# Four gate banks with a transpose each, and input products once per 16 steps, in a recurrent step of an LSTM-and-experts kernel

## The chip, the cores and the metric

One core of a Trainium2 chip runs the program. The metric is the device time of one execution in microseconds. Five engines work side by side, each in the order of its own instruction stream: TensorE (PE in the profile; its weight loads are listed as PEld), VectorE (DVE), ScalarE (ACT), GpSimd (POOL) and SyncE (SP, which here only starts DMAs). They wait for each other through semaphores. Matmul results land in PSUM, which has eight banks per partition; everything else lies in SBUF.

## The reference

The input `x` has shape (2, 1024, 256). An LSTM runs over its 1024 steps for both sequences, and a layer of experts runs on the result. Both add to `x`. All numbers are float32.

```python
xW = jnp.einsum('ntd,dk->tnk', x, Wx) + b              # gates in the order i, f, o, g
def step(carry, xw_t):
    prev_h, prev_c = carry
    a = xw_t + prev_h @ Wh                             # (2, 256) @ (256, 1024)
    i, f = sigmoid(a[:, :H]), sigmoid(a[:, H:2*H])
    o, g = sigmoid(a[:, 2*H:3*H]), tanh(a[:, 3*H:])
    next_c = f * prev_c + i * g
    next_h = o * tanh(next_c)
    return (next_h, next_c), next_h
x = x + hs                                             # h0 = cond_1024, c0 = 0
# then, on every token: two shared experts (SiLU gated, 512 wide) and eight routed
# experts (GELU, 256 wide), of which a router takes the best two
x = x + experts(x)
```

Each of the 1024 steps needs the `h` of the step before, so the steps can't overlap. The experts of a token need only that token's `h`.

## The kernel before

**The step.** The 256 hidden units are two halves, `m` = 0 and 1, of 128 units. A step is written out in the loop `for t in range(T)` (line 728). TensorE multiplies `h` by `Wh` in 32 products (line 747): for each of the 8 entries of `BLOCKS` (line 69) four products, one for each 32-row strip `q`. An entry is `(k, m, pair)`: which half of the old `h` is multiplied, which half of the units is made, and which two of the four gates. Every product is float32 and leaves two weight loads and two matmuls in the trace (32 columns of weights, 64 columns of moving data), so a step has 64 of each. The products of the half `m` accumulate into one PSUM bank `ps[m]`, 128x64.

**The window.** `h_window` hands TensorE 32 columns of which 2 are the two sequences' `h` and the others are zero, at a place that moves with the step. So one bank collects the rows of several steps, and products of other steps add zeros to them. In the kernel before, 16 of the 32 rows belong to one pair of gates and 16 to the other (`PAIR`), which gives 8 steps (`TH`) before a fresh bank is needed. `gates_ps` has two buffers for each half, so the next 8 steps' bank can be prepared.

**Input products.** `x @ Wx + b` is computed ahead for blocks of 128 steps into `inputs`. `inject` (line 654) adds it into a gate bank by a product with the identity: eight products for 8 steps, spread over the steps, into the next bank (`nxt`).

**After the products.** VectorE transposes each half's bank in 32x32 blocks within the same bank (`transpose`, line 787), which puts units on partitions. ScalarE then makes three gates with one sigmoid (line 790) and `g` with a tanh (line 791). VectorE computes `f*c` (line 794), copies `g` to a scratch tile `seen` so that the scan itself need wait for one semaphore only (line 798), and forms `c` with a scan (line 799). ScalarE makes `tanh(c)` (line 807), VectorE makes `h` (line 810). VectorE's order in a step is: both transposes; then `forget`, `seen`, scan of half 0; the same of half 1; then the two `h`.

**Fill.** The experts' work and the input products are queued in `Fill` as small units. `run_pe` gives TensorE some of them after the 32 products of a step, at most `ROOM` = 4 in cost (a 128x256 product with 256 tokens costs 2). `GROUPS` says how many steps' tokens go through the experts together, `PACES` over how many steps that work is spread. ScalarE's and VectorE's parts of it run at the end of a step within budgets (line 824: 1.0, line 835: 0.6). When no unit is left, a product `busy` of 128x256 on the identity may be issued; whether it is, is decided at the first step of each 8 (`spare`, line 760) and holds for the 8.

**Instruction counting.** `fill.issued` counts TensorE's instructions (4 per product, plus the extra wait instructions that `WAITS` lists by step). `inject` is moved and split so that a multiple of `FETCH` = 256 doesn't fall just at a step's start. The profile lists these fetches as a DMA queue of its own, `q8 instruction`.

**The end.** The last 32 steps' experts can only run when the loop is over (`last_shared_down`, `last_routed_down`, `last_add`, from line 502).

Of the kernel before, what the change touches and what calls it, by code (L numbers as in the profile page):

```python
# [16 lines left out]
P = 128  # L17
# [6 lines left out]
PAIR = ROWS // 2  # L24
TH = PAIR // N
TB = 2 * TH
# [9 lines left out]
GROUPS = [128] * 3 + [32] + [128] * 4 + [64, LAST]  # L36

PACES = [128] * 7 + [56, 31, 0]
# [9 lines left out]

FETCH = 256
EARLY = 16  # L50
WAITS = (
    1, 8, 16, 24, 32, 40, 48, 56, 64, 72, 80, 88, 96, 104, 112, 120, 128, 136, 144, 149,
    152, 157, 160, 160, 165, 168, 176, 181, 184, 189, 192, 197, 200, 208, 216, 224, 232,
    240, 248, 256, 264, 272, 280, 288, 296, 304, 312, 320, 328, 336, 344, 352, 360, 368,
    376, 384, 392, 400, 408, 416, 419, 421, 423, 424, 428, 430, 432, 435, 437, 439, 440,
    440, 447, 448, 456, 464, 472, 480, 488, 496, 504, 512, 520, 528, 529, 536, 544, 552,
    560, 568, 576, 584, 592, 600, 608, 616, 624, 632, 640, 648, 656, 664, 672, 680, 688,
    688, 696, 704, 712, 720, 728, 736, 744, 752, 760, 768, 776, 784, 792, 800, 808, 816,
    824, 832, 840, 848, 856, 864, 872, 880, 888, 896, 904, 912, 920, 928, 930, 933, 935,
    936, 940, 942, 944, 947, 949, 951, 952, 956, 958, 960, 963, 965, 968, 976, 984, 992,  # L60
    999, 1000, 1004, 1006, 1008, 1011, 1013,
# [6 lines left out]

BLOCKS = [
    (0, 0, 0), (0, 0, 1), (0, 1, 0), (1, 0, 0), (1, 0, 1), (0, 1, 1), (1, 1, 0), (1, 1, 1)  # L70
# [3 lines left out]
class Fill:  # L74
# [36 lines left out]
    def run(self, queue, budget):  # L111
        while queue and queue[0][0] <= self.step and queue[0][1] <= budget:
            _, cost, fn = queue.popleft()
            budget -= cost
            fn()

# [18 lines left out]
def lstm_moe_kernel(  # L135
# [106 lines left out]
    gates_ps = ctx.enter_context(tc.tile_pool(name="gates_ps", bufs=2, space=PSUM))  # L242
# [22 lines left out]
    behind = deque([(gates_ps, "ps0"), (fill_ps, "ps_f"), (gates_ps, "ps1")])  # L265
# [20 lines left out]
    def experts(t0, S):  # L286
# [215 lines left out]
        def last_shared_down(c):  # L502
            if c < 0:
                st["down"] = bank()
                x_kqj = st["down"][:W, 0, :].rearrange("p (q k j) -> p k q j", q=Q, k=K)
                for k in range(K):
                    product(
                        x_kqj[:, k], mov[k], ident_s,
                        start=(k == 0), stop=False, skip_group_check=True,
                    )  # L510
                return
            ps, n = st["down"], NS * HS // P
            for g in range(2):
                product(
                    ps[g * W : (g + 1) * W, 0, :], st["h_s"][:, c + g, :W], w2_sb[:, c + g, :],
                    start=(c + g == 1), stop=(c + 2 == n), skip_group_check=True,
                )
            if c + 2 == n:
                fill.to_dve(0.45, lambda: begin_sum(0, ps), lag=0)
# [12 lines left out]
        def last_add(e2, ps):  # L532
            acc = st["acc", 0]
            nc.vector.scalar_tensor_tensor(  # L534
                acc, ps[:, 0, :], st["gates"][:, e2 : e2 + 1], acc, ALU.mult, ALU.add
            )
            fill.let_go()
            if e2 == E // 2 - 1:
                both = bank()[:W, 0, :]
                product(both, fold, acc, start=True, stop=True)  # L540
                total = work.tile([P, D], F32, name="y")[:W]
                nc.scalar.activation(total, both, AF.Copy)  # L542
                nc.sync.dma_start(out=out_tn[t0 : t0 + S], in_=total)
# [40 lines left out]

# [11 lines left out]
    def h_window(t, k, pair):  # L596
        at = EDGE + t % TB * ROWS - N * (t % TH) - pair * PAIR
        return hs[t // TB % 2][:, k, at : at + ROWS]

# [7 lines left out]
    def pairs(blk):  # L607
        flat = blocks[blk].rearrange("p (h c) w -> p h (c w)", c=2)
        return flat.rearrange("p h (g c r) -> p h g c r", c=2, r=PAIR)

    def keep_inputs(blk, tile_, w0, w1, ps):
        h, c = divmod(tile_, 2)
        nc.scalar.activation(  # L613
            pairs(blk)[:, h, w0 // PAIR : w1 // PAIR, c, :],
            ps[:, : w1 - w0].rearrange("p (g r) -> p g r", r=PAIR),
            AF.Identity, bias=b_sb[:, tile_ : tile_ + 1],
        )
        made.update((blk, tile_, w) for w in range(w0, w1, PAIR))

# [34 lines left out]
    def inject(banks, grp, i, pieces=1):  # L654
        m, q = divmod(i, Q)
        blk, g = divmod(grp, XB // TH)
        assert all((blk, 4 * m + 2 * (q // 2) + c, g * PAIR) in made for c in range(2))
        for piece in range(pieces):
            w0, w1 = 64 * piece // pieces, 64 * (piece + 1) // pieces
            product(  # L660
                banks[m][0][q * ROWS : (q + 1) * ROWS, w0:w1],
                pairs(blk)[:, 2 * m + q // 2, g].rearrange("p c r -> p (c r)"),
                ident[:, q % 2 * 64 + w0 : q % 2 * 64 + w1],
                start=(piece == 0), stop=False, skip_group_check=True,
            )

    def gates_tile(m):

        a = gates_ps.tile([P, 4, P], F32, name=f"ps{m}")
        return a[:, 0, :64], a[:, 1, :64], a[:, 2:]  # L670
# [10 lines left out]

    ends, e0 = {}, 0
# [28 lines left out]
    nxt = [gates_tile(m) for m in range(K)]  # L711
    busy = nxt[0][2]
# [12 lines left out]
    for i in range(K * Q):  # L725
        inject(nxt, 0, i)
    due = 12
    for t in range(T):
        fill.step = t
        grp, u = divmod(t, TB)  # L730
        if t % TH == 0:
            cur, nxt = nxt, [gates_tile(m) for m in range(K)]
            ps, turned, busy = [a[0] for a in cur], [a[1] for a in cur], nxt[0][2]
            spare = False
# [10 lines left out]

        for k, m, pair in BLOCKS:
            for q in range(Q):
                w0 = q * D + m * P + pair * 64
                product(
                    ps[m][q * ROWS : (q + 1) * ROWS],  # L750
                    h_window(t, k, pair),
                    wh_sb[:, k, w0 : w0 + 64],
                    start=False,
                    stop=(t % TH == TH - 1 and k == K - 1 and pair == 1),
                    skip_group_check=True,
                )
        left = max(1, due - t)
        done = fill.run_pe(-(-len(fill.pe) // left), ROOM)
        if t % TH == 0:
            spare = not done  # L760
        if spare and not done:
            product(
                busy, ident, ident.unsqueeze(1).to_broadcast([P, 2, P]),
                start=(t % TH == 0), stop=False, skip_group_check=True,
            )

        if t // TH + 1 < T // TH:
            put = put if t % TH else 0
            fill.issued += WAITS.count(t)

            left = K * Q - put
            count = next(
                (n for n in range(max(0, t % TH + 1 - put), left + 1)
                 if -(fill.issued + 4 * n) % FETCH > EARLY), left)
            first = -(fill.issued + 4 * count) % FETCH
            for i in range(count):
                more = i == count - 1 and first <= EARLY
                inject(nxt, t // TH + 1, put, 2 + first // 4 if more else 1)
                put += 1

        rows = slice(N * (t % TH), N * (t % TH + 1))
        gates = [turned[m].rearrange("p (a r) -> p a r", r=PAIR)[:, :, rows] for m in range(K)]
        c_new = [cells[m][:, t % 2] for m in range(K)]
        seen = [stepp.tile([P, N], F32, name=f"seen{m}") for m in range(K)]

        def transpose(m):
            nc.vector.transpose(turned[m], ps[m])  # L787

        def squash(m):
            nc.scalar.activation(sgm[:, u, m, :, :, 1], gates[m][:, 0:3], AF.Sigmoid)  # L790
            nc.scalar.activation(gf[:, u, m, :, 0], gates[m][:, 3], AF.Tanh)  # L791
# [4 lines left out]
        def cell(m):  # L796

            nc.vector.tensor_copy(seen[m], gf[:, u, m, :, 0])  # L798
# [13 lines left out]
        for fn in (transpose, squash):  # L812
            for m in range(K):
                fn(m)
        for m in range(K):
            forget(m)
            cell(m)
            squash_cell(m)
        for m in range(K):
            output(m)  # L820
        if u == TB // 2 and t + TB < T:
            nxt_results = results()
        else:
            fill.run(fill.act, 1.0)
# [9 lines left out]
        if u < TB - 1:  # L834
            fill.run_dve(0.6)
            continue
# [91 lines left out]
```

## Time and profile before

| | us |
|---|---|
| median of 3 runs (2252.95 to 2262.92) | 2254.86 |
| the profiled execution, its own time | 2256.97 |
| span of its instructions, first to last | 2254.8 |
| TensorE busy, matmuls / weight loads | 2033.5 / 1484.8 |
| VectorE busy | 1571.3 |
| ScalarE busy | 909.5 |
| first transpose starts at | 10.16 |
| last `h` ends at | 2234.03 |

The mean granted TensorE clock is 0.996 of full speed. A matmul's duration in the trace includes the way through the array: the 64 matmuls of a step take 0.22 us each by their rows and yet are done in about 1.1 us together. "Busy 90%" of TensorE therefore says little about how much more it could take. What counts in this kernel is the length of one step, since 1023 of them follow each other between the first transpose and the last.

### The profile page before, as it was taken

The numbers are of one execution on the slowest core, as the hardware profiler recorded it, in microseconds if no ns is written. First come the engines' busy times: TensorE is split into PE (matmuls) and PEld (weight loads), VectorE is DVE, ScalarE is ACT, GpSimd is POOL, SyncE is SP. The second block draws the span as 40 slices with busy tenths as digits, with TensorE's granted clock in tenths as the row PEclk, the third lists the DMA queues.
The fourth block names the chain that finished last, engine by engine and source line by source line (L and its number), as shares of the span: only waits on it lengthen the run. The fifth ranks groups of instructions, "written<-read, shape, count | busy, mean of one in ns | idle before, by whom it ended". The sixth has DMA issues, their size and how long they took to land.

```text
span 2254.8 us, 159246 instructions
## 1 busy us (share of the span) xinstructions
PE 2033.5 (90%) x70612; PEld 1484.8 (66%) x70612; DVE 1571.3 (70%) x11041; ACT 909.5 (40%) x6487; POOL 2.7 (0%) x9
## 2 busy tenths in 40 slices
PE   8988899888989889998798899988898988989998
PEld 6666666666666666777666666666666666667787
DVE  5666667776777667777667767676676776667776
ACT  3334344433444334443344443444434344334443
POOL 0000000000000000000000000000000000000000
PEclk9999999999999999999999999999999999999999
DMA  2111100000000000000000000000000000000000
GB/s 65 35 35 35 35 28 5 5 5 7 7 5 5 5 7 7 5 7 7 5 6 5 5 5 7 7 4 5 5 7 7 4 5 5 7 7 5 5 9 7
DMA packets 15330, 23.84 MB, mean 11 GB/s; under 512 B 2864, under 2 KB 14128, under 8 KB 14640
## 3 DMA queue, kind: packets, MB, share of 16 engines
q1 hardware_dynamic: 14352, 12.62, 1.9%
q8 instruction: 552, 9.04, 1.7%
q14 instruction: 138, 1.13, 0.2%
q10 hardware_dynamic: 288, 1.05, 0.1%
HBM read 11.56 MB, written 2.10 MB: 6 GB/s over the span
## 4 chain that ended last, share of the span: by engine, by line
PE 61%; DVE 36%; issue 3%; DMA 0%; SPq 0%; ACT 0%
PE ps L255 53%; DVE ps L787 10%; DVE c L799 10%; PE ps_f L255 8%; DVE results L794 7%; DVE seen L798 6%; DVE h L810 3%; DMA wh_sb<-in_wh_dram 0%; SPq L165 0%; DVE acc L534 0%; SPq L173 0%; SPq L171 0%; SPq L170 0%; DVE acc L492 0%; ACT y L542 0%
## 5 line engine op out<-in xcount | busy, mean ns | idle before, releaser
L255 PE MATMUL ps<-wh_sb,h 128*32 128x64 f32 x65536 | 1143.8, 221 | 214.3 <-DVE h L810 210.5
L255 PEld LDWEIGHTS ps<-wh_sb,h 128*32 128x32 f32 x65536 | 975.1, 110 | 393.1 <-DVE h L810 386.8
L787 DVE STREAM_TRANSPOSE ps<-ps 128x64 f32<-128x64 f32 x2048 | 543.4, 265 | 498.5 <-PE ps L255 426.0
L790 ACT ACTIVATE results<-ps 128x6 f32<-128x6 f32 x2048 | 361.3, 176 | 1103.8 <-DVE ps L787 1009.4
L810 DVE TENSOR_TENSOR h<-results,c 128x2 f32<-128x2 f32 x2048 | 314.2, 153 | 168.4 <-ACT c L807 168.2
L807 ACT ACTIVATE c<-c 128x2 f32<-128x2 f32 x2048 | 321.5, 157 | 217.5 <-DVE c L799 181.7
L799 DVE TENSOR_TENSOR_SCAN c<-results 128x4 f32<-128x4 f32 x2048 | 358.2, 175 | 0.0
L791 ACT ACTIVATE results<-ps 128x2 f32<-128x2 f32 x2048 | 342.4, 167 | 0.0
L798 DVE COPY seen<-results 128x2 f32<-128x2 f32 x2048 | 332.8, 162 | 0.0
L794 DVE TENSOR_TENSOR results<-results,c 128x2 f32<-128x2 f32 x2048 | 319.3, 156 | 0.0
L255 PEld LDWEIGHTS ps<-ident,inputs 128*32 128x32 f32 x2090 | 124.0, 108 | 265.7 <-issue 228.4
L255 PE MATMUL ps<-ident,inputs 128*32 128x64 f32 (+2 forms) x2090 | 263.9, 230 | 0.3
L255 PE MATMUL ps_f<-x2T,w_sb 128*128 128x256 f32 (+3 forms) x640 | 173.4, 379 | 0.0
L255 PE MATMUL ps_f<-x2T,r_sb 128*128 128x256 f32 (+3 forms) x640 | 173.2, 378 | 0.0
L255 PE MATMUL ps_f<-r_sb,h_r 128*128 128x256 f32 (+1 forms) x520 | 165.9, 419 | 0.9 <-DVE acc L492 0.9
L255 PEld LDWEIGHTS ps_f<-x2T,r_sb 128*128 128x128 f32 (+1 forms) x640 | 88.5, 184 | 22.8
L255 PEld LDWEIGHTS ps_f<-x2T,w_sb 128*128 128x128 f32 (+1 forms) x640 | 86.7, 184 | 21.8 <-issue 0.2
L255 PEld LDWEIGHTS ps_f<-r_sb,h_r 128*128 128x128 f32 (+1 forms) x520 | 80.0, 184 | 23.3 <-DVE acc L492 1.3
L255 PE MATMUL ps_f<-xT_sb,wx_sb 128*128 128x256 f32 (+2 forms) x384 | 84.5, 346 | 0.3 <-ACT inputs L613 0.3
L255 PE MATMUL ps<-ident 128*128 128x256 f32 x232 | 82.8, 443 | 1.4 <-POOL ident masks.py:199 1.4
L255 PE MATMUL ps_f<-w_sb,h_s 128*128 128x256 f32 (+1 forms) x256 | 82.6, 419 | 0.0
L492 DVE SCALAR_TENSOR_TENSOR acc<-ps_f,gate,acc 128x256 f32<-128x256 f32 (+1 forms) x128 | 61.1, 478 | 1.2 <-PE ps_f L255 1.0
(87 smaller groups left out, 475.1 us busy)
## 6 DMA issues: line engine op xcount, KB each, us to landing
r_sb<-in_r_w1T_dram SPq DMA_DIRECT2D x16, 128.0 KB, 2.5
r_sb<-in_r_w2T_dram SPq DMA_DIRECT2D x16, 128.0 KB, 2.1
out_dram<-acc SPq DMA_DIRECT2D x15, 128.0 KB, 2.1
xT_sb<-in_xT_dram SPq DMA_DIRECT2D x14, 128.0 KB, 2.5
wx_sb<-in_wx_dram ACTq DMA_DIRECT2D x2, 512.0 KB, 4.3
wh_sb<-in_wh_dram SPq DMA_DIRECT2D x2, 512.0 KB, 6.2
w_sb<-in_s_w1T_dram SPq DMA_DIRECT2D x8, 128.0 KB, 2.2
w_sb<-in_s_w3T_dram SPq DMA_DIRECT2D x8, 128.0 KB, 2.2
```

The lines of the kernel that those rows point to most:

```text
L255: nc.tensor.matmul(*operands, **how)
L492: nc.vector.scalar_tensor_tensor(acc, ps, st["gate"][:, i, e : e + 1], acc, ALU.mult, ALU.add)
L787: nc.vector.transpose(turned[m], ps[m])
L790: nc.scalar.activation(sgm[:, u, m, :, :, 1], gates[m][:, 0:3], AF.Sigmoid)
L791: nc.scalar.activation(gf[:, u, m, :, 0], gates[m][:, 3], AF.Tanh)
L794: nc.vector.tensor_mul(gf[:, u, m, :, 1], sgm[:, u, m, 2, :, 1], c_prev[m][:, :, 1])
L798: nc.vector.tensor_copy(seen[m], gf[:, u, m, :, 0])
L799: nc.vector.tensor_tensor_scan(c_new[m].rearrange("p n z -> p (n z)"), sgm[:, u, m, 0].rearrange("p n z -> p (n z)"), gf[:, u, m].rearrang ...
L807: nc.scalar.activation(cells[m][:, 2, :, 0], c_new[m][:, :, 1], AF.Tanh)
L810: nc.vector.tensor_mul(h_cols(t + 1)[:, m], sgm[:, u, m, 1, :, 1], cells[m][:, 2, :, 0])
```

## The change

- **Four banks.** Each half has two gate banks, one for `f` and `g` (pair 0) and one for `i` and `o` (pair 1); `gates_ps` has one buffer of each. The host puts the gates in the order f, g, i, o (`early`).
- **No pairs in the rows.** All 32 rows of a bank belong to steps, so a bank serves 16 steps (`TB`). `TH`, `PAIR` and the buffer pairs `cur`/`nxt` are gone.
- **Order of the products.** `BLOCKS` now finishes the banks in the order (0, f g), (0, i o), (1, f g), (1, i o): after 3, 4, 6 and 8 of its entries. Old half 1 of `h` is needed from the third entry on (the fourth before).
- **Four transposes per step** instead of two, and VectorE's order becomes: transpose (0, f g), (0, i o), (1, f g), `forget(0)`, transpose (1, i o), scan of half 0, `forget(1)`, scan of half 1, the two `h`. The copies to `seen` are gone. In the built program each scan has a separate wait instruction ahead of it on VectorE, for its own engine's `forget`, while the scan itself waits for ScalarE's `i, o`.
- **ScalarE** has three activations per half instead of two: sigmoid of `f`, tanh of `g`, sigmoid of `i, o`.
- **Input products at once.** At the end of each 16th step all 16 `inject` products for the next 16 steps are issued, after at most half the usual fill.
- **Fill.** `busy` is issued in every step without fill. `ready_pe` counts what `run_pe` will issue. Groups and paces near the end, and the budgets of ScalarE and VectorE fill (0.9, 0.5), are changed.
- **Instruction counting.** `WAITS` lists about one extra wait per step, and after the fill small 32x32 products on the identity are added as padding (1436 in the built program) so that, one step ahead of the burst of input products, the next multiple of 256 is 72 to 140 instructions away.
- **The end.** The last expert sum is made, folded, copied and stored in two column halves; the residual of the last group is added by two products that lie on different rows.

The long `WAITS` table and blank lines are left out of the diff.

```diff
-TB = 2 * TH
+TB = ROWS // N
-GROUPS = [128] * 3 + [32] + [128] * 4 + [64, LAST]
-PACES = [128] * 7 + [56, 31, 0]
+GROUPS = [128] * 3 + [32] + [128] * 3 + [64] * 3 + [LAST]
+PACES = [128] * 6 + [60, 60, 48, 27, 0]
-EARLY = 16
+EARLY = 12
+STEP = 137
+FROM, UPTO = 72, 140
 BLOCKS = [
-    (0, 0, 0), (0, 0, 1), (0, 1, 0), (1, 0, 0), (1, 0, 1), (0, 1, 1), (1, 1, 0), (1, 1, 1)
+    (0, 0, 0), (0, 0, 1), (1, 0, 0), (1, 0, 1), (1, 1, 0), (0, 1, 0), (0, 1, 1), (1, 1, 1)
 ]
...
+    def ready_pe(self, count, room):
+        done, banks = 0, self.banks
+        for opens, cost, _ in self.pe:
+            if done == count or opens > banks or cost > room:
+                break
+            banks -= opens
+            room -= cost
+            done += 1
+        return done
...
-    gates_ps = ctx.enter_context(tc.tile_pool(name="gates_ps", bufs=2, space=PSUM))
+    gates_ps = ctx.enter_context(tc.tile_pool(name="gates_ps", bufs=1, space=PSUM))
...
-    def h_window(t, k, pair):
-        at = EDGE + t % TB * ROWS - N * (t % TH) - pair * PAIR
+    def h_window(t, k):
+        at = EDGE + t % TB * ROWS - N * (t % TB)
         return hs[t // TB % 2][:, k, at : at + ROWS]
...
-    def inject(banks, grp, i, pieces=1):
...
+    def inject(grp, m, pair):
+        blk, g = divmod(grp, XB // TB)
+        w = slice(g * ROWS, (g + 1) * ROWS)
+        for q in range(Q):
+            tile_ = 4 * m + 2 * (q // 2) + pair
             product(
+                ps[m][pair][q * ROWS : (q + 1) * ROWS], blocks[blk][:, tile_, w],
+                ident[:, q % 2 * 64 : q % 2 * 64 + 64],
+                start=True, stop=False, skip_group_check=True,
             )
...
+    banks = [
+        [gates_ps.tile([P, 4, P], F32, name=f"ps{m}{pair}") for pair in range(2)] for m in range(K)
+    ]
+    ps, turned = [[[a[:, j, :64] for a in b] for b in banks] for j in range(2)]
+    busy = banks[0][0][:, 2:]
...
         for k, m, pair in BLOCKS:
             for q in range(Q):
                 w0 = q * D + m * P + pair * 64
                 product(
+                    ps[m][pair][q * ROWS : (q + 1) * ROWS], h_window(t, k), wh_sb[:, k, w0 : w0 + 64],
+                    start=False, stop=(u == TB - 1 and (m, pair) in seen), skip_group_check=True,
                 )
...
-        for fn in (transpose, squash):
-            for m in range(K):
-                fn(m)
-        for m in range(K):
-            forget(m)
-            cell(m)
-            squash_cell(m)
+        transpose(0, 0)
+        squash(0)
+        transpose(0, 1)
+        squash_late(0)
+        transpose(1, 0)
+        squash(1)
+        forget(0)
+        transpose(1, 1)
+        squash_late(1)
+        cell(0)
+        squash_cell(0)
+        forget(1)
+        cell(1)
+        squash_cell(1)
         for m in range(K):
             output(m)
+        left = max(1, due - t)
+        count = -(-len(fill.pe) // left)
+        feeds = u == TB - 1 and t < T - 1
+        room = ROOM // 2 if feeds else ROOM
+        done = fill.ready_pe(count, room)
+        fill.run_pe(count, room)
+        if not done:
+            product(
+                busy, ident, ident.unsqueeze(1).to_broadcast(busy.shape),
+                start=False, stop=False, skip_group_check=True,
+            )
+        fill.issued += WAITS.count(t)
+        if feeds:
+            for m, pair in PAIRS:
+                inject((t + 1) // TB, m, pair)
+        to_go = (TB - 2 - u) % TB
+        then = -(fill.issued + to_go * STEP) % FETCH
+        short = -(-max(0, then - UPTO if then > UPTO else then + FETCH - UPTO if then < FROM else 0) // 4)
+        pads = -(-short // (to_go + 1)) if t < T - TB else 0
+        while pads or not EARLY < -fill.issued % FETCH < FETCH - 2:
+            product(
+                busy[:ROWS, 0, :ROWS], ident[:, :ROWS], ident[:, :ROWS],
+                start=False, stop=False, skip_group_check=True,
+            )
+            pads = max(0, pads - 1)
```

## The prediction

> **What bounds the kernel now.** I read first the list of costliest groups (which engine carries the step), then the chain of waits, then one undisturbed step in order of time, and last the steps that are longer than it. The chain's first line says that neither DMA nor ScalarE's or SyncE's own work fills it; it alternates between TensorE and VectorE:
>
> ```profile
> PE 61%; DVE 36%; issue 3%; DMA 0%; SPq 0%; ACT 0%
> ```
>
> One step, start and duration in us:
>
> ```profile
> 601.66 0.15 DVE L810 TENSOR_TENSOR h<-results,c 128x2 f32<-128x2 f32 x1
> ...
> 601.86 0.94 PEld L255 LDWEIGHTS ps<-wh_sb,h 128*32 128x32 f32 x64 [0.82 <-DVE h L810]
> ...
> 601.97 0.16 DVE L810 TENSOR_TENSOR h<-results,c 128x2 f32<-128x2 f32 x1 [0.16 <-ACT c L807]
> ...
> 602.69 0.60 DVE L787 STREAM_TRANSPOSE ps<-ps 128x64 f32<-128x64 f32 x2 [0.42 <-PE ps L255]
> ...
> 602.99 0.18 ACT L790 ACTIVATE results<-ps 128x6 f32<-128x6 f32 x1 [1.05 <-DVE ps L787]
> 603.07 0.17 ACT L791 ACTIVATE results<-ps 128x2 f32<-128x2 f32 x1
> 603.20 0.16 DVE L794 TENSOR_TENSOR results<-results,c 128x2 f32<-128x2 f32 x1
> 603.27 0.16 DVE L798 COPY seen<-results 128x2 f32<-128x2 f32 x1
> ...
> 603.39 0.17 DVE L799 TENSOR_TENSOR_SCAN c<-results 128x4 f32<-128x4 f32 x1
> ...
> 603.60 0.16 ACT L807 ACTIVATE c<-c 128x2 f32<-128x2 f32 x1
> ...
> 603.73 0.17 DVE L799 TENSOR_TENSOR_SCAN c<-results 128x4 f32<-128x4 f32 x1
> 603.81 0.15 DVE L810 TENSOR_TENSOR h<-results,c 128x2 f32<-128x2 f32 x1
> ```
>
> From `h` to `h` it is 2.15 us (2.153 by the exact starts of most steps). TensorE starts 0.05 after `h` of half 0, the first transpose 0.83 later, and `h` 1.12 after that. The first transpose is at 10.165, the last pair at 2232.44: 1023 steps of 2.172 on average, so 19.7 us in all lie above 2.153. Three views show where:
>
> ```profile
> 40.80:51.00 10.20, 8.07 (x230) 6.55 (x222) 4.78 (x37) 2.61 (x20) 0.00 (x0) 0.53 0.11 30
> ```
>
> This stage ran at about half the granted clock (0.53, third number from the end). Its steps 13 to 17 took 3.3 us more than five of 2.153; two like it (at 1471 and 1751) took 1.1 each: **5.5 us**.
>
> ```profile
> 1773.61 0.27 DVE L787 STREAM_TRANSPOSE ps<-ps 128x64 f32<-128x64 f32 x1 [0.17 <-PE ps L255]
> ...
> 1774.15 0.14 PEld L255 LDWEIGHTS ps<-wh_sb,h 128*32 128x32 f32 x3 [0.45 <-issue]
> ...
> 1774.49 0.27 DVE L787 STREAM_TRANSPOSE ps<-ps 128x64 f32<-128x64 f32 x1 [0.62 <-PE ps L255]
> 1774.66 0.14 DVE L794 TENSOR_TENSOR results<-results,c 128x2 f32<-128x2 f32 x1
> ```
>
> Here TensorE waited for nothing that the profile names, in the middle of the step's products. Counting TensorE's instructions, 30 such gaps (0.10 to 0.56 us) lie exactly where a new block of 256 begins, together **8.3 us**: instruction fetch. The same rows give the spacing of a transpose: the next VectorE instruction starts 0.17 after it, though it lasts 0.27.
>
> **The new step, in ns from its first transpose.** Hops read from the starts of a clean step: VectorE end to ScalarE start 33, ScalarE to VectorE 35, `h` to TensorE 52. VectorE starts its next ready instruction 84 to 92 before the end of the last: 72 after a TENSOR_TENSOR, 82 after a scan, 174 after a transpose. A scan waiting for its own engine starts 36 after that end; with a separate wait instruction ahead it is 37 + 66 = 103 (in the row of three L492 sums at 2234.14 the second starts 0.10 after the first one's end, the third 0.04 after the second's; the built program has that wait ahead of the second).
>
> TensorE: step 0 shows a restart in the middle:
>
> ```profile
> 9.66 0.60 PEld L255 LDWEIGHTS ps<-wh_sb,h 128*32 128x32 f32 x40 [0.57 <-DMA wh_sb<-in_wh_dram]
> ...
> 10.16 0.60 DVE L787 STREAM_TRANSPOSE ps<-ps 128x64 f32<-128x64 f32 x2 [2.68 <-PE ps L255]
> ```
>
> 0.500 from load to transpose with 16 loads between; the second transpose 0.334 later for 24 more, 13.9 each. The new step restarts at its 17th load, when `h` of half 1 arrives. Bank (0, f g) is complete 8 loads later: first transpose at 500 - 112 = 388 after the restart, the other banks 112, 335 and 558 after it.
>
> - Transposes: 0; 174; 348 (its bank at 335); then `forget(0)` at 522 (its sigmoid: 298, 465, +35 = 500); transpose (1, i o) at 594 (its bank at 558).
> - Scan 0: `forget(0)` ends 678, +103 = 780. `forget(1)` 862, ends 1018. Scan 1: 1018 + 103 = 1121 (its sigmoid of `i, o`: 594 + 265 + 33 = 892, ends 1064, +35 = 1099: waits 22 less).
> - `tanh` of half 1: 1121 + 174 + 33 = 1328; `h` 1519, ends 1675; TensorE restarts 1727; next first transpose **2115**.
> - `h` of half 0 stands behind scan 1: 1203, ends 1355, TensorE 1407. Its 16 loads take 195, so TensorE then stands 125 waiting for half 1. That is its cover.
>
> So removing two copies and adding two transposes costs VectorE time, and the gain is that half 0's gates no longer wait for 40 loads: 2115 against 2153, **1023 x -38 = -38.9 us**. Each ns of transpose spacing moves the step by 3 (both `forget`s and scan 1 stand behind three of them); at 187 the gain is gone.
>
> A rule stands against this row. The Trainium skill, "VectorE: DVE Perf Modes", section "The DRAIN you can't avoid", says that the next VectorE operation doesn't start until the pipe is empty. By it a transpose would hold the next for its 265, the walk would give 2467 a step and the sum some 2578 us. The row at 1774.66 has 174, and the row decides.
>
> **What else changes.**
>
> - *Clock.* In the built program before, 19 steps have neither fill nor `busy`; 12 to 15, 671 and 799 just ahead of the slow clock are among them. Afterwards there are none: **-5.5** (0 if it drops anyway).
> - *Fetch.* Before, 72 blocks begin among `h` products less than 4.0 us after the one before (by the order of the instructions, at 2.153 a step) and lose 0.107 each; 403 come later and lose 0.0016. The new program has 129 of the first kind, counted in the same way at 2.115. 62 of them follow the burst of input products, two steps on at load 27, and come some 0.5 us closer than before; I take 0.2 for these (between 0.107 and 0.6), 0.107 for 67: 19.6, less 8.3 = **+11**. Ends: 0 and 129 x 0.5 - 8 = +57.
> - *Full steps.* With two 256-wide products of fill TensorE's own time rules:
>
> ```profile
> 1001.05 0.97 PEld L255 LDWEIGHTS ps<-wh_sb,h 128*32 128x32 f32 x64
> ...
> 1002.11 0.73 PEld L255 LDWEIGHTS ps_f<-w_sb,h_s 128*128 128x128 f32 x4
> ...
> 1003.17 0.14 PEld L255 LDWEIGHTS ps<-ident,inputs 128*32 128x32 f32 x2 [0.33 <-ACT c L807]
> ```
>
>   1.06 + 1.06 = 2.12, and 0.04 for small products behind it, as here until 1003.21. 174 new steps are so full, 122 with padding: 122 x 0.045 + 52 x 0.005 = **+5.7** (0 to +14, if padding costs 0.1). Before, this was covered by 2.153.
> - *Burst.* 1.06, one fill product 0.63, 32 loads 0.45, 0.02 for padding: 2.16 in 63 steps: **+2.8** (0 to +8). The last four wait for the sigmoid of bank (1, i o), which ends before their turn.
> - *VectorE fill* had 0.72 from `h` to the transpose and has 0.60; the longest takes 0.48 - 0.08 = 0.40 after 0.07: hidden. *ScalarE* has one activation more per half, inside its waits: hidden.
> - *End.* Three L492 sums and 8 weight loads of the group before follow the last `h`, and the last group's first product comes at 2236.60. With the new pace that group's products are issued by step 1019: **-2** (0 to -3). The split at the end is inside this.
>
> Sum against the profiled execution: 2256.97 - 38.9 - 5.5 + 11.3 + 5.7 + 2.8 - 2 = 2229.4; the median of the runs lies 2.1 lower: **2227**.
>
> **Rivals.**
>
> 1. *The separate waits don't bind* (the sigmoid of half 1 does, at 1099): 22 less a step, 2205. For it: only 22 ns apart. Against: the wait sits in the same stream as its `forget`. 0.12.
> 2. *Instruction fetch becomes the bound of the burst.* The burst puts some 200 instructions into one step, so the next block is wanted earlier; before, the largest gap was 0.56. At 0.56 in all 129 places: 72 - 8 = +64 in place of 11, 2280. It turns slower from 0.36 each (47 us, which is 39 more than before). For it: it is the only stall that grows with a shorter step. Against: 39 of the 72 short intervals before show none. 0.14.
> 3. *A transpose doesn't let a transpose start early.* Only TENSOR_TENSOR behind a transpose is shown. At 200 ns: 26 x 3 = 78 more a step than forecast, 2307; from 187 the step is no shorter than before. 0.06.
> 4. *TensorE rules most steps, not 174*, by tile changes between fill, padding and products: the step stays near 2.15, about 2250. Single-fill steps need 1.06 + 0.63 + 0.04, so 0.4 is spare. 0.08.
>
> The forecast itself has 0.60, with 2208 to 2245. A measurement here tells from about 0.5% (11 us). Faster: 0.58 of the forecast, 0.12 of rival 1 and little else, 0.71; slower: rival 3, half of rival 2, some of 4: 0.17; same 0.12. The range takes rival 1 with less fetch at the low end and half of rival 2 at the high end: 2196 to 2264.
>
> **What would show it.** Right: clean steps of 2.10 to 2.13; VectorE's first two transposes 0.17 apart; scan 1 0.10 after `forget(1)` ends; a pause of 0.1 before the 17th load; no stage at half clock. Wrong: transposes 0.2 or more apart, or gaps at "issue" of 0.3 and more in the step after next behind each burst.

## The result: 1.1% slower, by instruction fetch

| | before | after |
|---|---|---|
| median of 4 runs, us | 2255.32 (2252.95 to 2262.92) | 2279.56 (2276.78 to 2290.74) |
| ratio to before (95% interval) | | 1.0111 (1.0070 to 1.0152) |
| profiled span, us | 2254.8 | 2278.1 |
| first transpose, us | 10.165 | 9.893 |
| step, most steps, us | 2.153 | 2.095 |
| step, mean of 1023, us | 2.172 | 2.191 |
| from the end of the last `h` to the end, us | 20.8 | 24.8 |

The forecast was 2227, in a range of 2196 to 2264. The two rows on the step hold the story: a step that nothing disturbs became 0.058 us shorter, more than forecast, and the mean step still became 0.019 longer. All the times in this section and below that are finer than a row shows are taken from the starts of the instructions in the trace.

The undisturbed step first. Timeline of the kernel after, start and duration in us:

```profile
603.14 0.15 DVE L851 TENSOR_TENSOR h<-results,c 128x2 f32<-128x2 f32 x1
...
603.34 1.04 PEld L324 LDWEIGHTS ps<-wh_sb,h 128*32 128x32 f32 x64
...
604.05 0.60 DVE L827 STREAM_TRANSPOSE ps<-ps 128x64 f32<-128x64 f32 x3 [0.35 <-PE ps L324]
...
604.56 0.15 DVE L837 TENSOR_TENSOR results<-results,c 128x2 f32<-128x2 f32 x1
604.63 0.26 DVE L827 STREAM_TRANSPOSE ps<-ps 128x64 f32<-128x64 f32 x1
...
604.81 0.17 DVE L840 TENSOR_TENSOR_SCAN c<-results 128x4 f32<-128x4 f32 x1
604.89 0.15 DVE L837 TENSOR_TENSOR results<-results,c 128x2 f32<-128x2 f32 x1
...
605.15 0.17 DVE L840 TENSOR_TENSOR_SCAN c<-results 128x4 f32<-128x4 f32 x1
605.23 0.15 DVE L851 TENSOR_TENSOR h<-results,c 128x2 f32<-128x2 f32 x1
```

From `h` to `h` 2.09. The 64 weight loads last 1.04 where the row of before had 0.94: the pause before the 17th load is in it. Three transposes take 0.60 together, so they overlap as the walk had it; the scan of half 1 stands 0.26 behind the start of its `forget`.

Now what ate it. The list of groups of weight loads, first the kernel before, then the kernel after (count | busy us, mean ns | idle time ahead of them and what ended it):

```profile
L255 PEld LDWEIGHTS ps<-wh_sb,h 128*32 128x32 f32 x65536 | 975.1, 110 | 393.1 <-DVE h L810 386.8 <-issue 4.3 <-DMA wh_sb<-in_wh_dram 0.6
```

```profile
L324 PEld LDWEIGHTS ps<-wh_sb,h 128*32 128x32 f32 x65536 | 1017.8, 109 | 250.3 <-DVE h L851 110.6 <-issue 57.6 <-DMA wh_sb<-in_wh_dram 0.6
```

"issue" is time in which TensorE waited for nothing that the profile names: 4.3 us before, 57.6 after. Counted by TensorE's instructions as in the prediction, 114 gaps over 0.095 us lie inside the `h` products at the place where a block of 256 begins, together 68.0 us; before there were 30 with 8.3. They are not spread evenly. With u the step's place in its 16 (the burst of input products ends u = 15), the mean step is 2.828 at u = 1 and 2.327 at u = 6; no other is above 2.22. The two make (0.733 + 0.232) x 64 = 62 us. One step u = 1, kernel after:

```profile
1345.13 0.57 PEld L324 LDWEIGHTS ps<-wh_sb,h 128*32 128x32 f32 x27 [0.22 <-DVE h L851]
...
1345.84 0.27 DVE L827 STREAM_TRANSPOSE ps<-ps 128x64 f32<-128x64 f32 x1
...
1346.50 0.59 PEld L324 LDWEIGHTS ps<-wh_sb,h 128*32 128x32 f32 x37 [0.80 <-issue]
...
1346.86 0.49 DVE L827 STREAM_TRANSPOSE ps<-ps 128x64 f32<-128x64 f32 x2 [0.75 <-PE ps L324]
```

27 loads, then nothing for 0.80, then the other 37. `h` has long been there; the second transpose waits for TensorE, and the step lasts 3.00. This is the gap of "0.3 and more in the step after next behind each burst" that the prediction named as what would prove it wrong.

The end of the kernel, after:

```profile
2253.10 0.16 DVE L851 TENSOR_TENSOR h<-results,c 128x2 f32<-128x2 f32 x1 [0.17 <-ACT c L848]
2253.57 2.04 DVE L564 SCALAR_TENSOR_TENSOR acc<-ps_f,gate,acc 128x256 f32<-128x256 f32 x4
...
2254.63 5.41 PE L324 MATMUL ps_f<-r_sb,h_r 128*128 128x256 f32 x16 [1.74 <-DVE acc L564]
...
2259.96 0.41 PE L324 MATMUL ps<-wr_sb,x2T 128*64 128x8 f32 x8
```

16 of these instructions of the group before the last are still to come after the last `h` (before: 8, in 1.99 us), they wait for a bank that four sums hold, and they run in a stage of lower clock (0.68 as the mean of 2254.6 to 2260). The last group's first product starts 6.7 us after the end of `h`, against 2.6.

### The profile page after: what moved, and what is told of

It reads as the page before. It is cut to its first block, busy times and chain, and to the rows that moved or that the text cites. A ratio compares the mean times of both kernels' runs of the same rounds, so it can differ in the third digit from the quotient of the medians.

```text
span 2278.1 us, 170316 instructions
## 1 busy us (share of the span) xinstructions
PE 2157.1 (95%) x73638; PEld 1603.6 (70%) x73638; DVE 1620.3 (71%) x11067; ACT 1085.2 (48%) x8537; POOL 2.7 (0%) x9
## 4 chain that ended last, share of the span: by engine, by line
PE 72%; DVE 20%; issue 6%; ACT 2%; DVEq 0%; DMA 0%; SPq 0%; ACTq 0%
PE ps L324 53%; PE ps_f L324 19%; DVE ps L827 11%; DVE c L840 5%; DVE results L837 2%; DVE h L851 1%; ACT results L830 1%; ACT results L831 0%; DVEq L840 0%; ACT results L834 0%; DMA wh_sb<-in_wh_dram 0%; ACT c L848 0%; DVE acc L564 0%; SPq L234 0%; ACT er L512 0%
## 5 line engine op out<-in xcount | busy, mean ns | idle before, releaser
L324 PE MATMUL ps<-wh_sb,h 128*32 128x64 f32 x65536 | 1241.1, 222 | 99.0 <-issue 40.9
L324 PEld LDWEIGHTS ps<-wh_sb,h 128*32 128x32 f32 x65536 | 1017.8, 109 | 250.3 <-DVE h L851 110.6
L827 DVE STREAM_TRANSPOSE ps<-ps 128x64 f32<-128x64 f32 x4096 | 864.7, 254 | 354.2 <-PE ps L324 314.7
L830 ACT ACTIVATE results<-ps 128x2 f32<-128x2 f32 x2048 | 352.5, 172 | 909.9 <-DVE ps L827 878.0
L324 PEld LDWEIGHTS ps<-ident 128*32 128x32 f32 (+1 forms) x3170 | 208.3, 117 | 300.3 <-ACT results L834 157.6
L834 ACT ACTIVATE results<-ps 128x4 f32<-128x4 f32 x2048 | 357.0, 174 | 56.7 <-DVE ps L827 38.0
L324 PE MATMUL ps<-ident 128*32 128x32 f32 (+1 forms) x3170 | 359.9, 224 | 13.6 <-POOL ident masks.py:199 1.4
L831 ACT ACTIVATE results<-ps 128x2 f32<-128x2 f32 x2048 | 342.3, 167 | 0.0
L837 DVE TENSOR_TENSOR results<-results,c 128x2 f32<-128x2 f32 x2048 | 308.3, 151 | 1.7 <-ACT c L848 1.7
L324 PEld LDWEIGHTS ps_f<-x2T,w_sb 128*128 128x128 f32 (+1 forms) x704 | 93.8, 184 | 22.7 <-PE ps L324 0.9
L518 DVE SCALAR_TENSOR_TENSOR h_r<-er,ps_f 128x256 f32<-128x256 f32 x126 | 52.3, 415 | 0.6 <-ACT er L512 0.6
```

Of the source, the lines that this page charges most:

```text
L324: nc.tensor.matmul(*operands, **how)
L518: nc.vector.scalar_tensor_tensor(st["h_r"][:, c + i : c + j, :W], er[:, i:j], 1.0, ps[:, i:j], ALU.add, ALU.mult)
L827: nc.vector.transpose(turned[m][pair], ps[m][pair])
L830: nc.scalar.activation(sgm[:, u, m, 2, :, 1], gates[m][0][:, 0], AF.Sigmoid)
L831: nc.scalar.activation(gf[:, u, m, :, 0], gates[m][0][:, 1], AF.Tanh)
L834: nc.scalar.activation(sgm[:, u, m, :2, :, 1], gates[m][1], AF.Sigmoid)
```

## The experiments

Two theories stood against each other: that blocks of instructions arrive too late for TensorE (fetch), or that the burst itself (16 products, the restart of four banks) makes what follows late. The runs below were on two other chips, on each of which the kernel before took 2250, not 2255; so they are compared by their ratio to it. The kernel after was not run there; by its ratio it would be 1.0111 x 2250 = 2275, with an interval of 9 us each way.

**e1: the same work, blocks begin elsewhere**

```diff
-FROM, UPTO = 72, 140
+FROM, UPTO = 72, 80
```

> The window for the start of a block in the burst step is narrowed from 72-140 to 72-80 instructions: the same work, 64 padding products more, and the blocks of 256 start some 60 instructions earlier. Fetch theory: the 0.73 us by which the step two on from the burst (u = 1) is longer than 2.095 vanishes there, and comes back in the step right behind the burst (u = 0), where a block then starts at load 60, by the starts of the instructions 2.5 us after the one before instead of 3.1: 1.0 to 1.2 us a burst; u = 11 takes over the 0.23 of u = 6, at 0.5. In all 33 to 50 us more than 2279.6: 2312 to 2330. Rival (the burst itself, its products or its restart of the four banks, makes what follows late): u = 1 stays 0.7 too long and the time stays at 2275 to 2285.

Measured: 2275.17 us, ratio 1.0116 (1.0099 to 1.0133). The stall moved to the steps that fetch names: u = 1 fell from 2.828 to 2.111, u = 6 from 2.327 to 2.116, u = 0 rose from 2.203 to 2.960 and u = 11 from 2.123 to 2.230. The step behind the burst, timeline of e1:

```profile
1339.30 0.95 PEld L324 LDWEIGHTS ps<-wh_sb,h 128*32 128x32 f32 x61
...
1340.92 0.14 PEld L324 LDWEIGHTS ps<-wh_sb,h 128*32 128x32 f32 x3 [0.67 <-issue]
...
1341.26 0.27 DVE L827 STREAM_TRANSPOSE ps<-ps 128x64 f32<-128x64 f32 x1 [0.66 <-PE ps L324]
```

Now 61 loads run, and the last 3 wait 0.67. The burst is the same as before, so it is not the burst that stops TensorE in the step after next. The size was missed: a sum of 33 to 50 us more was expected, and there is none (within those 9 us). In e1 the block ahead of the stall begins among `h` products, not in the burst; its transfer of instructions then starts 0.92 us after that and has landed at 1.99 (medians of 64), while behind a start in the burst it was 1.18 and 2.37 (63). So the stall from the shorter interval (2.56 instead of 2.97, medians of all stalled places) is 0.87 instead of 0.73, not 1.0 to 1.2. In both places TensorE goes on some 1.4 us after the landing. Why a transfer starts later behind the burst stays open.

**e2: no padding for the place of the blocks**

```diff
-        pads = -(-short // (to_go + 1)) if t < T - TB else 0
+        pads = 0
```

> No padding products to bring the blocks into step with the burst (1290 of 1436 are gone; the rule on the last 12 instructions of a step stays), so that blocks start at every place of the step in turn. Fetch theory: half of the bursts have a stall in the step behind them and half in the one after, the 0.23 at u = 6 goes, and 23 blocks fewer are fetched: 15 to 30 us less than 2279.6, 2250 to 2265. Rival (the burst itself): u = 1 stays at 2.8 us in nearly all groups, the padding was 1290 x 0.02 hidden under VectorE, 2275 to 2282.

Measured: 2229.97 us, ratio 0.9913 (0.9898 to 0.9927): 45 us less than the kernel after by the ratios, more than expected. The stalls at block starts fell by 46, so the 1290 padding products themselves cost nothing that shows. u = 0 takes 2.313 and u = 1 2.278, so the stall is shared between the two, and u = 6 is down to 2.108. The padding, which was to bring the blocks into step with the burst, put the stall into nearly every group (62 of 64) at the same bad place.

**e3: no fill in the burst step**

```diff
-        room = ROOM // 2 if feeds else ROOM
+        room = 0 if feeds else ROOM
...
-        if not done:
+        if not done and not feeds:
```

> The burst step issues no fill product and no busy product; they go to the next steps. Fetch theory: the block that starts in the burst starts 0.3 us earlier (the burst then waits for the gates' activations, not for fill), so the stall two steps on shrinks by about that: 0.3 x 62 = 19 us at most, with the 0.08 of u = 15 another 4 us; 2258 to 2275. Rival (the burst itself): only the 0.08 of u = 15 goes, 2275, and u = 1 stays at 2.83.

Measured: 2254.14 us, ratio 1.0018 (1.0009 to 1.0027). u = 1 goes from 2.828 to 2.645 (12 us in 64 groups), u = 15 from 2.217 to 2.109 (7 us); the rest, 5 us by the two traces, are small parts of other steps. The block in the burst begins earlier, and the stall two steps on is shorter by 0.18, not by the full 0.3.

**e4: padding by a list**

```diff
-        to_go = (TB - 2 - u) % TB
...
-        while pads or not EARLY < -fill.issued % FETCH < FETCH - 2:
+        for _ in range(PADS.count(t)):
             product(
                 busy[:ROWS, 0, :ROWS], ident[:, :ROWS], ident[:, :ROWS],
```

The list `PADS` stands in place of the rule and of the `WAITS` table; a step has 0 to 8 padding products by it.

> The rule for padding is replaced by a list, 534 products instead of 1436, set so that a block starts as seldom as possible among the step's h products less than 3.6 us after the one before (92 such places, 36 of them under 3.2, against 117 and 88). Nothing else differs. Fetch theory: 28 to 40 us less than 2279.6: 2240 to 2252, a little faster than the kernel before (2255), with the clean step still 2.095. Rival (the burst itself): 2275 to 2282.

Measured: 2220.09 us, ratio 0.9870 (0.9855 to 0.9885): 1.3% faster than the kernel before, and 20 us below the range expected (15, when the range is moved to a chip where the kernel before takes 2250). Its clean step is 2.100 in half of the steps and 2.096 in a quarter. The groups of weight loads, e1 to e4 in order:

```profile
L324 PEld LDWEIGHTS ps<-wh_sb,h 128*32 128x32 f32 x65536 | 1016.6, 109 | 239.3 <-DVE h L851 83.5 <-issue 54.1 <-DMA wh_sb<-in_wh_dram 0.2
```

```profile
L324 PEld LDWEIGHTS ps<-wh_sb,h 128*32 128x32 f32 x65536 | 1008.8, 110 | 585.9 <-DVE h L851 520.2 <-issue 19.5 <-ACT results L834 0.8
```

```profile
L324 PEld LDWEIGHTS ps<-wh_sb,h 128*32 128x32 f32 x65536 | 1017.3, 109 | 227.0 <-DVE h L851 101.9 <-issue 36.4 <-ACT results L831 1.1
```

```profile
L285 PEld LDWEIGHTS ps<-wh_sb,h 128*32 128x32 f32 x65536 | 1005.8, 110 | 532.0 <-DVE h L812 483.8 <-issue 3.8 <-DMA wh_sb<-in_wh_dram 0.9
```

The "issue" term runs 57.6, 54.1, 19.5, 36.4, 3.8 from the kernel after to e4, and the ratios 1.0111, 1.0116, 0.9913, 1.0018, 0.9870 follow it: from after to e4 it falls by 54 us, and 0.0241 x 2250 is 54 too; from after to e3 by 21, and 0.0093 x 2250 is 21. Less close are e2 (38 for 45 us) and e1 (3.5 for none). Counted one by one, as the 68.0 was, the stalls at block starts sum to 68.0, 62.1, 22.1, 47.1 and 5.0 us. The same step as shown above, 609, in e4:

```profile
1309.02 1.04 PEld L285 LDWEIGHTS ps<-wh_sb,h 128*32 128x32 f32 x64 [0.67 <-DVE h L812]
...
1309.73 0.60 DVE L788 STREAM_TRANSPOSE ps<-ps 128x64 f32<-128x64 f32 x3
```

All 64 loads in one row, at 1.04. The five profiles (after, e1 to e4) together give the stall as a function of the time between the starts of two blocks. Counted are blocks that begin among `h` products behind the 17th load; the interval is taken without the stall itself, and the stall is what the gap has over the usual 0.014 between two loads:

| interval, us | under 2.6 | 2.6-2.9 | 2.9-3.2 | 3.2-3.5 | 3.5-3.8 | 3.8-4.1 | over 4.1 |
|---|---|---|---|---|---|---|---|
| blocks | 56 | 35 | 304 | 79 | 73 | 845 | 465 |
| mean stall, us | 0.84 | 0.66 | 0.35 | 0.27 | 0.05 | 0.013 | 0.005 |

The interval alone doesn't decide. Each start of a block is followed by one transfer in the queue of instructions (579 and 579 in the kernel after), and when that transfer lands says more. All blocks among `h` products in all ten profiles, by the time from this landing to the moment at which the next block is wanted:

| landing to wanted, us | under 0.6 | 0.6-0.8 | 0.8-1.0 | 1.0-1.2 | 1.2-1.4 | 1.4-1.6 | over 1.6 |
|---|---|---|---|---|---|---|---|
| blocks | 96 | 71 | 100 | 148 | 256 | 420 | 3675 |
| mean stall, us | 0.96 | 0.69 | 0.50 | 0.27 | 0.07 | 0.011 | 0.005 |

The 483 stalls over 0.095 us all end 1.19 to 1.65 us after the landing (median 1.41), and none of the 3675 blocks in the last column has such a stall. So TensorE waits there for its next block of instructions. What the 1.4 us are spent on no run shows.

**e5: the bank of f and g complete 8 loads later** (on e4, as all that follow)

```diff
-    (0, 0, 0), (0, 0, 1), (1, 0, 0), (1, 0, 1), (1, 1, 0), (0, 1, 0), (0, 1, 1), (1, 1, 1)
+    (0, 0, 0), (0, 0, 1), (1, 0, 1), (1, 0, 0), (1, 1, 0), (0, 1, 0), (0, 1, 1), (1, 1, 1)
```

> On e4: the two blocks of products behind the restart change places, so that half 0's bank of f and g is complete 16 loads after the restart instead of 8 (the bank of i and o 8 instead of 16). Nothing else differs. If the shorter step comes from f and g being transposed early, as the walk has it, everything from the first transpose on is 0.112 later: clean step 2.095 + 0.11 = 2.205, 1023 x 0.112 = 115 us more, less up to 20 that the longer step gives back in fetch and late starts: 2315 to 2335. Rival (the gain comes from the copies that are gone, and the order of the banks matters little): 2220 to 2240.

Measured: 2322.70 us, ratio 1.0323 (1.0306 to 1.0340), clean step 2.205. VectorE's rows of one step in e5:

```profile
602.45 0.53 DVE L788 STREAM_TRANSPOSE ps<-ps 128x64 f32<-128x64 f32 x3 [0.55 <-PE ps L285]
602.95 0.16 DVE L798 TENSOR_TENSOR results<-results,c 128x2 f32<-128x2 f32 x1
...
603.55 0.17 DVE L801 TENSOR_TENSOR_SCAN c<-results 128x4 f32<-128x4 f32 x1
```

From the first transpose on everything has its old distance (`forget` 0.50 behind it, the second scan 1.10); the first transpose itself is 0.112 later. So the 0.112 by which half 0's f and g come earlier is the step's in full: this is where the shorter step comes from. Without it the step is 0.052 longer than in the kernel before, so the rest of the change costs time. And the three transposes, whose banks are now all complete in time, take 0.53: the third starts 0.131 behind the second.

**e6: TensorE restarts at its 25th load**

```diff
-    (0, 0, 0), (0, 0, 1), (1, 0, 0), (1, 0, 1), (1, 1, 0), (0, 1, 0), (0, 1, 1), (1, 1, 1)
+    (0, 0, 0), (0, 0, 1), (0, 1, 0), (1, 0, 0), (1, 0, 1), (1, 1, 0), (0, 1, 1), (1, 1, 1)
```

> On e4: a third block that needs only half 0 is put ahead of the restart, so that TensorE waits for half 1 at its 25th load instead of its 17th, 0.014 instead of 0.125. The walk: half 0's banks are complete at the same distance from the restart, the last bank 0.112 earlier, which nothing uses: clean step 2.095 to 2.107. But a TensorE that comes late to a step (fill, a block that starts in the padding) now delays the step from 0.014 on instead of from 0.125: in e4's trace the late starts add up to 45 us over 0.014 and 19 us over 0.125. So the cover is worth 26 us, less up to 8 of gaps among the products that the earlier last bank hides: 2238 to 2252. Rival (late starts are made up elsewhere, the pause is slack without use): 2212 to 2225.

Measured: 2237.85 us, ratio 0.9941 (0.9923 to 0.9960), at the low edge of what was expected, and not by the way expected. In e6 the 64 loads take 0.94, the pause is gone:

```profile
603.53 0.94 PEld L285 LDWEIGHTS ps<-wh_sb,h 128*32 128x32 f32 x64 [0.78 <-DVE h L812]
```

But the clean step is 2.108: the first transpose comes 0.403 after the 25th load, where it came 0.388 after the 17th. That alone is 8 us of the 17 by which the mean step grew (2.134 to 2.150), counted from e4's most frequent step, 2.100, and 13 from 2.095. Another 4 are stalls at block starts (8.8 us against e4's 5.0). So the pause as a cover is worth some 4 us here at most, not 18 to 26. What the 0.015 is was not followed.

**e7: the busy product made small**

```diff
             product(
-                busy, ident, ident.unsqueeze(1).to_broadcast(busy.shape),
+                busy[:ROWS, 0, :ROWS], ident[:, :ROWS], ident[:, :ROWS],
                 start=False, stop=False, skip_group_check=True,
```

> On e4: in the steps without fill the busy product (128 columns of weights, 256 of data) is one of 32 by 32, with as many instructions, so that no block of 256 moves. Clock theory: the stages at half clock come back, the first 52 steps without fill among them: one such stage of 10.24 us cost 3.3 us before, so 3 to 20 us more than 2220 (2223 to 2240), and the profile shows a granted clock near 0.5 between 30 and 140 us. Rival (the steps before only happened to fall into a slow stage): 2216 to 2222 and no more half-clock stages than e4 has.

Measured: 2234.21 us (2223.70 to 2235.97), ratio 0.9919 (0.9892 to 0.9946): 14 us more than e4 in the middle run. Stretches of 120 us, e7 (after the busy times: the granted clock, the DMA share, GB/s):

```profile
20.00:140.00 120.00, 90.08 (x3801) 71.62 (x3800) 76.93 (x576) 56.16 (x451) 0.00 (x0) 0.96 0.11 32
200.00:320.00 120.00, 94.33 (x3758) 76.39 (x3758) 77.11 (x573) 56.27 (x449) 0.00 (x0) 0.90 0.12 34
```

and e4:

```profile
20.00:140.00 120.00, 108.45 (x3869) 76.63 (x3869) 78.77 (x595) 57.39 (x464) 0.00 (x0) 1.00 0.11 33
200.00:320.00 120.00, 109.95 (x3889) 78.73 (x3885) 78.40 (x591) 57.51 (x462) 0.00 (x0) 0.99 0.12 34
```

Without the large product the clock falls to means of 0.96 and 0.90, and in the first stretch TensorE gets through 3801 matmuls where e4 does 3869. The trace's clock records have eleven stages at half clock among e7's steps, of 3.4 to 13.7 us, and two of 3.4 in e4; the steps in them stand 19.1 and 3.7 us above clean ones, a difference of 15, near the 14 by which the time is longer. So the busy product is what mostly holds the clock; e4, which has it in every step without fill, still has a stage at 313.5. The stages were shorter and more scattered than the "near 0.5 between 30 and 140" that was expected.

**e8: e4's padding made anew for e3's program**

```diff
-PADS = (
-    9, 9, 9, 9, 9, 9, 9, 9, 22, 22, 27, 40, 40, 40, 40, 40, 40, 40, 40, 41, 41, 41, 41,
...
+PADS = (
...
-        room = ROOM // 2 if feeds else ROOM
+        room = 0 if feeds else ROOM
...
-        if not done:
+        if not done and not feeds:
```

> e4 with its own list of padding (516 products) for a program whose burst steps issue no fill and no busy product. Fetch theory: the 0.07 of u = 15 goes (4.6 us), the rest stays: 0.984 to 0.987 of the kernel before, 2212 to 2220 where that takes 2250. Rival (fill moved to other steps makes TensorE late there): 0.987 to 0.990.

Measured: 2221.01 us, ratio 0.9871 (0.9853 to 0.9888), the same as e4. u = 15 falls from 2.167 to 2.110, but 185 steps instead of 146 now hold two large fill products, and these cost 14 us above the clean step instead of 10: the work is moved, not saved. The new list is also worse at its own task: the stalls at block starts sum to 11.4 us, against 5.0 in e4.

## Why the prediction was wrong, step by step

| term, us | predicted | measured | how |
|---|---|---|---|
| the step's walk | -38.9 | -59.3 | 1023 x (2.095 - 2.153) |
| fetch among `h` products | +11.3 | +59.7 | gaps of 68.0 less 8.3 |
| clock | -5.5 | -5.5 | before's 11 steps in slow stages stood 5.5 over clean ones; what comes of them after (2.6, one stage) is in the next row |
| full steps, burst, other late starts | +8.5 | +24.6 | what is left |
| end | -2 | +4.0 | 24.8 less 20.8 |
| start | 0 | -0.3 | first transpose |
| sum | -26.6 | +23.2 | 2278.1 - 2254.8 |

The terms of the prediction add up to 2230.4; its 2229.4 was a slip of 1.0 in the sum. Its 2578 for a step of 2467 leaves out the other terms, which are 12.3 together.

- **The step that failed is the price of fetch.** The prediction counted the places nearly right: 129 blocks among `h` products at short intervals (the trace has 125 under 3.8 us), 62 of them two steps behind the burst at about load 27, which is where the 0.80 stands in the trace. It then took 0.2 for each of these and 0.107 for each of the rest; the runs show 0.78 and less than that elsewhere, 68.0 us in place of 19.6.
- **Why 0.2 and 0.107 were the wrong price.** The 0.107 is the mean of places that were wanted later and served sooner: of the 72 in the trace of before, 57 are wanted 3.2 to 3.5 us after the block before began, their transfers land at 2.05 (median), and 47 of the 72 lose less than 0.1. The 62 are wanted at 2.97 and their transfers land at 2.37; with 1.41 from landing to use that makes a stall of 0.81, and the trace has 0.78 (0.73 as the mean over the 64 groups). At u = 6 the mean loss is 0.23. The shorter interval is only half of it: the 13 places of before that are wanted sooner than 3.2 lose 0.11 each, because their transfers land at 1.55. The trace of before has the rule (its 28 stalls over 0.095 us end 1.26 to 1.52 us after the landing), but how late a transfer lands behind a burst of 16 input products, which that kernel doesn't have, is not in it. So the rival "instruction fetch becomes the bound of the burst", given 0.14, is what came. That its 0.56 in all 129 places (72 us) lies close to the 68 measured is luck: the places of u = 1 lose more and most others less.
- **The transposes let each other start, as the row said.** The spacing is 0.174, 0.161, and 0.131 in e5, with durations of 0.22 to 0.27. The prediction held the Trainium skill's "VectorE: DVE Perf Modes", section "The DRAIN you can't avoid", against the row. That section also says that a next operation that is not held starts earlier, so it need not contradict the row; no transpose in a clean step here holds VectorE's next operation for the whole time that it lasts.
- **The clean step was mis-sized by 20 ns,** to the good. The walk put the third transpose 174 behind the second, at 348; it starts with its bank, at 335, and `forget(0)` at 508 instead of 522. Each scan starts 254 after its `forget` instead of 258. That carries through to 2095. The separate waits do bind, as the forecast had it: the scan of half 1 starts 58 ns after the sigmoid it needs has ended, so rival 1 was not what made the step shorter.
- **The cover of 0.125 before the 17th load** is there (0.126) and hides little: e6.
- **The clock term** had the right cause: the mean clock after is 0.999, and e7 shows what the busy product mostly prevents. "No stage at half clock" was too much: one of 3.4 us lies near the start and one behind the last step.
- **Full steps and burst** cost more than forecast, 24.6 by difference. It is not the place of the blocks: above 1023 clean steps and without the gaps, the kernel after has 30.5 us (98.5 less 68.0) and e4, which has few stalls, about as much, 34.7 (39.7 less 5.0). Of e4's, some 10 lie in steps with two large fill products and 4 in the burst step; the rest is spread over the other steps, in part because most of e4's steps take 2.100 and not 2.095. That last part was not traced further.
- **The end** went the other way: the group before the last is not done by step 1019, as had been assumed, but leaves 16 instructions instead of 8, and a stage of lower clock falls on them (5.41 us; e4 has 3.72 for the same 16).

What the experiments leave: the shorter clean step is worth 59 us (54 by e4's 2.100), and the place of the blocks decides whether it is kept. With the padding placed by a list (e4) the kernel takes 0.987 of the kernel before.

## What to carry to other kernels

In a long unrolled program with a dense instruction stream, write down for each block of 256 instructions of an engine the time at which it begins. Where the next begins sooner than some 3.7 us later and on the path, a stall can stand there; how long it is depends on when the transfer of instructions lands, which the trace has. A few cheap instructions elsewhere can move such a place into a wait. A mean stall from one set of places is no price for places that come closer together or behind denser work. A pattern that brings blocks to the same place in each round is a gain only where that place is good; at a bad place it is paid in each round, here 62 times.

## What the runs showed of the hardware

- A block of TensorE instructions was there 3.3 to 4.2 us after the block before it had begun (stalled places of the kernel after, 5th to 95th percentile, median 3.75), and 1.19 to 1.65 us (median 1.41, 483 stalls in ten profiles) after the transfer that followed that beginning had landed. This fits a fetch that asks for one block ahead. The Trainium skill, "Runtime: NRT & Kernel Launch", section "Instruction fetch mechanics", has the blocks of 256 and calls the cost of crossing one "mostly hidden"; here it was 68 us of 2278, with 579 blocks in the queue's row:

```profile
q8 instruction: 579, 9.49, 1.8%
```

- This transfer started 0.7 to 1.6 us after the block before began (kernel after, 5th to 95th percentile, median 1.1) and took 1.1 us itself (median).
- A transpose of 64 columns let the next one start 0.174 us later when it lasted 0.27, and 0.131 later when it lasted 0.22 (first and second of a step in e5).
- With small products in place of `busy`, TensorE did some work in every step and the mean clock still fell to 0.90 over 120 us (e7).
